# Turning the first stage's normed rows in by VectorE and DRAM instead of TensorE, in a one-core decoder layer

## The chip, the cores and the metric

One core of a Trainium2 chip runs the whole layer. The metric is the device time of one execution in microseconds. The core has five engines that each work through a queue of instructions in order: PE (TensorE, with PEld for its weight loads), DVE (VectorE), ACT (ScalarE), POOL (GpSimd) and SP (SyncE, which here only issues DMAs). They meet at semaphores.

## The reference

The input x has 16 x 256 tokens of 256 channels in float32. Three sublayers follow each other, each ending in a layer norm of `x + sublayer(x)`:

```python
# 1: attention to a fixed table, squared ReLU in place of a softmax (4 heads of 64)
n = layernorm(x) * ln_g + ln_b
q = n.reshape(B, T, 4, 64).transpose(0, 2, 1, 3)
k = w_fc.reshape(-1, 64); v = w_proj.T.reshape(-1, 64)      # 1024 x 64
p = square(relu(einsum('bhtd,sd->bhts', q, k)))
x = norm(x + (x + einsum('bhts,sd->bhtd', p, v)))
# 2: cross attention, 16 heads of 16, to ctx; a bias per head from clipped differences of `frac`
D = clip(frac[:, None, :] - frac[:, :, None], -0.2, 0.2)
attn = gamma * (Q @ K.T) / 4 + delta * (alpha_pos * max(D, 0) + alpha_neg * min(D, 0))
x = norm(x + (softmax(attn) @ V) @ Wo.T + bo)
# 3: FFN, 256 -> 1024 -> 256, with one of eight small LoRA updates chosen per token
x = norm(x + ffn(x))
```

## The kernel before

The order of work is written out by hand, and each engine's queue follows the program text. The first sublayer is the first stage. It works on eight blocks `tb` of 512 tokens, `rows_in[tb]`. The second stage (cross attention of 16 batches with the FFN of earlier blocks woven in) starts when it is through.

A block's x lies as four row tiles of 128 tokens by 256 channels. To be multiplied with the keys, the normed rows must stand with channels on the partitions. The steps for that, all done for block `tb + 1` while block `tb` is in its matmuls:

- `load` (L262) fetches x with one DMA of 512 KB; `measure` (L191, L192) takes mean and variance of the rows on DVE.
- `scale` takes the logarithm and exponential on ACT (L200, L202), and then four small DVE operations (L208 to L211, L246) for 1/std and the shift. It works on the sums of eight row tiles at once: four of the coming block, and four of an earlier block's result.
- `norm_in` (L251) writes the normed rows `xn` on ACT, four operations of 128x256.
- `turn_in(c)` turns them by eight 128x128 matmuls with an identity on TensorE (L326) into PSUM, and copies them out with `ln_g` and `ln_b` applied, on ACT for c = 0 (L330) and on DVE for c = 1 (L335), as `xnT`.

The matmuls of a block run in eight steps m, four for each half c of the channels. In a step, `scores` (L345) makes two `ps_a` tiles of 128x1024; ACT takes their ReLU into `pr` (L353), DVE squares it (L354). Then `values` (L364) multiplies the squares of the step before with the value table and adds up in two tiles of PSUM. There are two `ps_a` tiles in all, so the scores of a step need the ReLUs of the step before to be through; `pr` has four.

After each half, `keep` copies the sums out on ACT (L373, L378) and adds them on POOL (L379) as `xt`. The result of block `tb - 1` is turned back to rows by `turn_rows`: eight transposes on TensorE (L390) into a `ps_a` tile, and two DVE operations that add 2x (L396) into `y`. `measure_out` takes its statistics and `norm_out` writes the normed rows on ACT (L251) and adds a bias on POOL (L419).

Work besides the matmuls is listed in `steps[m]` and issued after the matmuls of step m. `turn_in`, `turn_rows` and the second half of `turn_in` stand in the list `turning` after step 7, that is at the boundary between two blocks:

```python
steps[6].append(lambda tb=tb: nxt.norm_in(by[tb]))
turning.append(lambda: nxt.turn_in(0))
if tb:
    turning.append(rows_in[tb - 1].turn_rows)
turning.append(lambda: nxt.turn_in(1))
```

Three side jobs lie in this stage. `clip` makes `dneg` and `dpos` of the first five batches, ten operations of 128x512 on DVE (L547) in blocks 2 to 6, at steps 0 and 5; those of batches 2 to 4 go to DRAM (L566). `biases` folds constants in block 1, with matmuls in PSUM tiles `ps_b` (L153, L160, L167). `load_cross` and `load_ffn` fetch the weights of the later sublayers during block 0.

`tile_b` hands out the `ps_b` tiles, two in turn. The second stage already has, for half of the heads of its later groups, another way of turning: `blocks` turns 32x32 blocks with a DVE operation (L707), writes them to DRAM (L712), and `fetch` reads them back in another order (four DMAs, L724).

Of the kernel before, what the change touches and what calls it, by code (L numbers as in the profile page):

```python
# [14 lines left out]
P = 128  # L15
# [7 lines left out]
def tile_decoder_layer(ctx: ExitStack, tc: tile.TileContext, a: dict, out: bass.AP):  # L23
# [214 lines left out]
    if True:  # L238
# [16 lines left out]
        class Block:  # L255
# [16 lines left out]
            def norm_in(self, by):  # L272
                self.xn = p1.tile([P, 4, C], FP, tag="xn", bufs=1, name="xn")
                for j in range(4):
                    scaled(self.xn[:, j, :], self.x[:, j, :], by, j)

            def begin(self):

                self.xn = p1.tile([P, 4, C], FP, tag="xn", bufs=1, name="xn")
                self.xnT = p1.tile([P, CC, 512], FP, tag="xnT", bufs=1, name="xnT")  # L280
                self.mv = small.tile([P, 4, 2], FP, tag="mv", name="mv")
                near, by = [], []
                for jj in range(2):
                    self.measure(jj)
                    near.append(near_root(self.mv[:, 2 * jj : 2 * jj + 2], 2))
                for jj in range(2):
                    mv = self.mv[:, 2 * jj : 2 * jj + 2]
                    by.append(scaling_of(mv, newton(mv, near[jj], 2), 2))
                for j in (0, 2, 1, 3):
                    rs, nm = by[j // 2]  # L290
                    if j < 2:
                        scaled(self.xn[:, j, :], self.x[:, j, :], (rs, nm), j)
                    else:
                        k = j - 2
                        nc.vector.tensor_scalar(
                            self.xn[:, j, :], self.x[:, j, :], rs[:, k : k + 1],
                            nm[:, k : k + 1], ALU.mult, ALU.add,
                        )
# [19 lines left out]
                        ln_b[:, c : c + 1], ALU.mult, ALU.add,  # L318
                    )

            def turn_in(self, c):
                if c == 0:
                    self.xnT = p1.tile([P, CC, 512], FP, tag="xnT", bufs=1, name="xnT")
                ps = tile_b()
                for j in range(4):
                    nc.tensor.transpose(  # L326
                        ps[:, j * P : (j + 1) * P], self.xn[:, j, c * P : (c + 1) * P], ident
                    )
                if c == 0:
                    nc.scalar.activation(  # L330
                        self.xnT[:, c, :], ps, AF.Identity,
                        bias=ln_b[:, c : c + 1], scale=ln_g[:, c : c + 1],
                    )
                else:
                    nc.vector.tensor_scalar(  # L335
                        self.xnT[:, c, :], ps, ln_g[:, c : c + 1], ln_b[:, c : c + 1],
                        ALU.mult, ALU.add,
                    )

            def scores(self, c, n):  # L340

                hf, q = divmod(n, 4)
# [1 line left out]
                for h, k in ((0, 0), (1, 1), (0, 1), (1, 0)):  # L344
                    nc.tensor.matmul(  # L345
                        sc[64 * k : 64 * k + 64, h, :],
                        lhsT=kT[64 * h : 64 * h + 64, q, hf * P + 64 * k : hf * P + 64 * k + 64],
                        rhs=self.xnT[64 * h : 64 * h + 64, c, :],
                        start=True,
                        stop=True,  # L350
                    )
                pr = p1.tile([P, 2, 512], FP, tag="pr", bufs=4, name="pr")
                nc.scalar.activation(pr, sc, AF.Relu)  # L353
                nc.vector.tensor_tensor(pr, pr, pr, ALU.mult)  # L354
                return pr

            def values(self, c, n, pr):
# [12 lines left out]
                    )  # L370

            def keep(self, c, last=False):
                nc.scalar.copy(self.oT[:, c, :], self.acc[0])  # L373
                if last:
                    nc.vector.tensor_tensor(self.oT[:, c, :], self.oT[:, c, :], self.acc[1], ALU.add)
# [51 lines left out]
    if True:  # L427
# [8 lines left out]
        class Batch:  # L436
# [119 lines left out]

            def clip(self, name):

                t = self.cut(name, *((0.0, -CLAMP) if name == "dneg" else (CLAMP, 0.0)))
# [453 lines left out]
    with tc.manual_schedule():  # L1013
# [21 lines left out]
        def scale(tb, mv):  # L1035
            by[tb] = scaling(mv, 8)

        for tb in range(NB):
            now = rows_in[tb]
            steps = [[] for _ in range(8)]  # L1040

            mv = small.tile([P, 8, 2], FP, tag="mv8", bufs=2, name="mv8")
            if tb in (0, 1, NB - 1):
                nc.vector.memset(mv, 0.0)

            if tb > 1:
                last = rows_in[tb - 2]
                last.mv = mv[:, 4:8]
                for jj in range(2):
                    steps[1 + jj].append(lambda jj=jj: last.measure_out(jj))  # L1050
                for j in range(4 if tb + 1 == NB else 1):
                    steps[7 - j // 2].append(
                        lambda j=j, tb=tb: last.norm_out(by[tb], 4 + j, j, nc.gpsimd)
                    )
            if tb > 2:
                older = rows_in[tb - 3]
                for j in range(1, 4):
                    steps[j].append(
                        lambda j=j, tb=tb: older.norm_out(by[tb - 1], 4 + j, j, nc.gpsimd)
                    )  # L1060
            turning = []
            if tb + 1 < NB:
                nxt = rows_in[tb + 1]
                nxt.mv = mv[:, 0:4]
                if tb:
                    steps[0].append(nxt.load)
                for jj in range(2):
                    steps[3 + jj].append(lambda jj=jj: nxt.measure(jj))
                steps[6].append(lambda tb=tb: nxt.norm_in(by[tb]))
                turning.append(lambda: nxt.turn_in(0))  # L1070
                if tb:
                    turning.append(rows_in[tb - 1].turn_rows)
                turning.append(lambda: nxt.turn_in(1))
            if tb + 1 < NB or tb > 1:
                steps[5].append(lambda tb=tb, mv=mv: scale(tb, mv))
# [22 lines left out]
            for m in range(8):  # L1098
# [334 lines left out]
```

## Time and profile before

| | |
|---|---|
| median of 3 runs (lowest to highest) | 887.35 us (887.11 to 888.24) |
| profiled execution, time | 887.49 us |
| profiled execution, span | 885.70 us |
| PE busy | 862.4 us, 97% of the span |
| DVE, ACT, POOL busy | 78%, 65%, 53% |
| first stage: `scores`, 1024 records (L345) | 124.6 us busy |
| first stage: `values`, 1024 records (L364) | 122.7 us busy |
| turning in (L326), 56 transposes | 8.6 us busy |
| turning out in this stage (L390 into `ps_a`), 48 transposes | 6.2 us busy |

Busy time is a union: pieces that overlap on an engine count once. The mean duration of an instruction is longer than its share, since matmuls overlap each other (a matmul of `scores` takes 593 ns from start to end, while 16 of them start within 1.72 us). The order of instructions on an engine and what each waited for is read from the timeline; `[0.95 <-ACT pr L353]` behind a row means that the engine had been idle 0.95 us and that ACT's instruction of line 353 released it.

### The profile page before, as it was taken

To read this page: it belongs to the slowest core of one execution; us is meant where nothing else is said; L and a number is where in the kernel's file an instruction comes from. 1 tells how busy PE (TensorE), PEld (TensorE's weight loads), DVE (VectorE), ACT (ScalarE), POOL (GpSimd) and SP (SyncE) were. 2 spreads that over 40 slices of the span, in tenths; PEclk is the share of its full clock that TensorE was granted. 3 is DMA by queue.
4 is the path that set the end of the run, shared out by engine and by line. 5 is a ranking of instruction groups with operands and counts; after the bars stand their busy time and mean duration, and the time that the engine had idled before them with its cause. 6 is when DMAs were issued, how large, how long until landed. Compare 5 with 4: busy or idle time off the path is not lost.

```text
span 885.7 us, 20853 instructions
## 1 busy us (share of the span) xinstructions
PE 862.4 (97%) x7708; PEld 513.1 (58%) x7708; DVE 693.3 (78%) x1975; ACT 577.0 (65%) x1012; POOL 466.6 (53%) x455
## 2 busy tenths in 40 slices
PE   8999999999999999999999999999999999999997
PEld 4334444444456776567547656754765675576655
DVE  6878899889779898769778877877887787777444
ACT  5766777777788788647747765774875577475111
POOL 1100223322479898656828765883976678374010
PEclk9999999999999999999999999999999999999999
DMA  5501101010001333454454536445453644642001
GB/s 139 159 1 43 54 24 44 31 49 1 8 8 48 99 98 110 139 162 149 158 155 150 158 129 184 151 155 168 138 164 133 193 151 135 181 149 102 28 7 41
DMA packets 70373, 92.94 MB, mean 105 GB/s; under 512 B 13824, under 2 KB 55296, under 8 KB 70272
## 3 DMA queue, kind: packets, MB, share of 16 engines
q1 hardware_dynamic: 69696, 91.35, 33.2%
q8 instruction: 61, 1.00, 0.5%
q14 instruction: 40, 0.33, 0.1%
q10 hardware_dynamic: 576, 0.26, 0.1%
HBM read 50.43 MB, written 39.58 MB: 102 GB/s over the span
## 4 chain that ended last, share of the span: by engine, by line
PE 44%; DVE 11%; issue 2%; POOL 1%; ACT 1%; DMA 0%; ACTq 0%; POOLq 0%; DVEq 0%
PE ps_l L945 9%; PE ps_b L978 6%; PE ps_l L664 5%; PE ps_v L764 5%; PE ps_b L743 4%; DVE neg L682 3%; PE ps_b L614 3%; PE ps_v L978 3%; PE ps_b L477 2%; PE ps_l L958 2%; DVE z L707 1%; PE ps_b L503 1%; PE ps_b L532 1%; POOL neg L733 1%; DVE dpos L547 1%
## 5 line engine op out<-in xcount | busy, mean ns | idle before, releaser
L682 DVE CUSTOM_DVE_ANT_0 neg<-ps_l,neg 128x256 f32<-128x256 f32 x512 | 181.5, 420 | 41.4 <-PE ps_l L664 38.3
L642 POOL TENSOR_SCALAR neg<-dneg,aneg,delta 128x512 f32<-128x512 f32 x252 | 198.9, 804 | 20.9 <-PE ps_b L743 10.0
L654 ACT ACTIVATE ps_l<-dpos,apos_d 128x512 f32<-128x512 f32 x256 | 172.2, 688 | 49.9 <-DVE mx L682 30.9
L354 DVE TENSOR_TENSOR pr<-pr 128x1024 f32<-128x1024 f32 x128 | 153.8, 1243 | 30.2 <-ACT pr L353 29.8
L733 POOL TENSOR_TENSOR neg<-neg,mx 128x1024 f32<-128x1024 f32 x65 | 124.0, 1909 | 85.4 <-DVE mx L682 84.3
L353 ACT ACTIVATE pr<-ps_a 128x1024 f32<-128x1024 f32 x128 | 125.0, 1026 | 53.0 <-PE ps_a L345 52.7
L345 PE MATMUL ps_a<-xnT,kT 64*64 64x512 f32 x1024 | 124.6, 593 | 1.0 <-ACT xnT L330 0.4
L364 PE MATMUL ps_v<-pr,vv 64*64 64x512 f32 x1024 | 122.7, 589 | 0.0
L945 PE MATMUL ps_l<-xt,wi 128*128 128x512 f32 x248 | 111.7, 596 | 0.2
L750 ACT ACTIVATE pT<-ps_b 128x512 f32<-128x512 f32 x160 | 87.4, 590 | 32.4 <-PE ps_b L743 30.9
L743 PE MATMUL ps_b<-ident,neg 128*128 128x128 f32 x640 | 87.1, 277 | 3.4 <-ACT pT L750 2.3
L743 PEld LDWEIGHTS ps_b<-ident,neg 128*128 128x128 f32 x640 | 71.5, 141 | 24.0 <-issue 6.2
L364 PEld LDWEIGHTS ps_v<-pr,vv 64*64 64x64 f32 x1024 | 45.0, 133 | 64.5 <-issue 54.6
L379 POOL TENSOR_TENSOR xt<-xt,half 128x512 f32<-128x512 f32 x15 | 19.1, 1274 | 119.8 <-ACT half L378 119.8
L419 POOL TENSOR_TENSOR hid<-hid,bo 128x256 f32<-128x256 f32 x32 | 43.6, 1366 | 71.8 <-ACT hid L251 71.8
L696 ACT ACTIVATE neg<-neg,mx 128x256 f32<-128x256 f32 x192 | 81.3, 498 | 0.0
L764 PE MATMUL ps_v<-pT,vaug 128*32 128x256 f32 x1024 | 74.3, 385 | 7.2 <-DVE x L991 6.0
L664 PE MATMUL ps_l<-kM,qT 32*64 32x256 f32 x2048 | 79.8, 388 | 0.0
L345 PEld LDWEIGHTS ps_a<-xnT,kT 64*64 64x64 f32 x1024 | 41.9, 133 | 65.3 <-issue 52.5
L945 PEld LDWEIGHTS ps_l<-xt,wi 128*128 128x128 f32 x248 | 45.6, 191 | 49.4 <-issue 44.6
L978 PE MATMUL ps_b<-wof,hT 128*128 128x256 f32 x304 | 68.4, 380 | 0.0
L524 POOL TENSOR_SCALAR kM<-keys,of_head 128x512 f32<-128x512 f32 x22 | 38.7, 1760 | 48.4 <-DVE keys L513 48.4
(137 smaller groups left out, 1183.3 us busy)
## 6 DMA issues: line engine op xcount, KB each, us to landing
pT<-away_z SPq DMA_DIRECT2D x192, 128.0 KB
away_z<-z SPq DMA_DIRECT2D x24, 512.0 KB
away_z<-kT SPq DMA_DIRECT2D x24, 512.0 KB
away_v<-raw SPq DMA_DIRECT2D x16, 512.0 KB
cT<-in_ctxT SPq DMA_DIRECT2D x16, 256.0 KB
v<-away_v SPq DMA_DIRECT2D x32, 128.0 KB
invs<-rows SPq DMA_DIRECT2D x16, 256.0 KB
x<-in_x SPq DMA_DIRECT2D x7, 512.0 KB
```

The lines of the kernel that those rows point to most:

```text
L345: nc.tensor.matmul(sc[64 * k : 64 * k + 64, h, :], lhsT=kT[64 * h : 64 * h + 64, q, hf * P + 64 * k : hf * P + 64 * k + 64], rhs=self.xnT[ ...
L353: nc.scalar.activation(pr, sc, AF.Relu)
L354: nc.vector.tensor_tensor(pr, pr, pr, ALU.mult)
L364: nc.tensor.matmul(self.acc[k][64 * h : 64 * h + 64, :], lhsT=vv[64 * k : 64 * k + 64, hf, 64 * q : 64 * q + 64], rhs=pr[64 * k : 64 * k + ...
L642: nc.gpsimd.tensor_scalar(self.neg[:, g], self.batch.dneg, aneg[:, h : h + 1], delta, ALU.mult, ALU.mult,)
L654: nc.scalar.activation(banks[g], self.batch.dpos.rearrange("p j k -> p (j k)"), AF.Copy, scale=apos_d[:, h : h + 1],)
L664: nc.tensor.matmul(banks[g][64 * h : 64 * h + 64, j * S : (j + 1) * S], lhsT=self.batch.qT[rows, self.o, j * P + 64 * h : j * P + 64 * h + ...
L682: nc.vector.tensor_tensor_reduce(out=self.t[:, g, j, :], in0=banks[g][:, j * S : (j + 1) * S], in1=self.neg[:, g, j, :], scale=-1.0 if min ...
L733: eng.tensor_tensor(rows, rows, top.to_broadcast([P, 4, S]), ALU.subtract)
L743: nc.tensor.transpose(ps[:, k * S + j * P : k * S + (j + 1) * P], self.t[:, g, j, k * P : (k + 1) * P], ident,)
L945: nc.tensor.matmul(self.banks[g], lhsT=wi[:, c, f * P : (f + 1) * P], rhs=self.xT[:, c, :], start=(c == 0), stop=False,)
L978: nc.tensor.matmul(ps[:, 0:C], lhsT=self.hT[f][:, j * P : (j + 1) * P], rhs=wof[:, f, :], start=(f == 0), stop=(f == FC - 1),)
```

## The change

The first block is turned in as before, by `turn_first`. For the other seven, `turn_in` is gone. A normed block is turned in 32x32 blocks by one DVE operation of 128x1024 (`blocks_in`), written to DRAM by one DMA and read back by four, into `xr`. Then ACT applies `ln_g` and `ln_b` in place, two operations of 128x512 (`affine`). In `xr` the tokens of a block stand in another order (by 32s), so `scores` reads it in four pieces of 128 tokens, and `keep` puts the tokens back in order as it copies.

The list of steps is laid anew. `measure` of the next block moves to steps 0 and 1, `scale` to step 2, `norm_in` to steps 2 and 3 in halves, `blocks_in` to step 4, `affine` to step 6. The load of x is issued half a block earlier, in step 4 of the block before. `turn_rows` moves from the boundary to step 3 of the next block and takes two `ps_b` tiles in place of a `ps_a` tile. `measure_out` stands in steps 5 and 6, `norm_out` in steps 5 and 7. The tile of sums has three buffers, and `xnT` two. `load_ffn` moves from block 0 to block 1, step 6.

One of the sixteen squares of a block, that of c = 0, n = 3, goes from DVE to ACT. The clips of the first five batches go from DVE to POOL, three operations for each.

```diff
+            def norm_in(self, by, jj):
+                if jj == 0:
+                    self.xn = p1.tile([P, 4, C], FP, tag="xn", bufs=1, name="xn")
+                for j in range(2 * jj, 2 * jj + 2):
+                    scaled(self.xn[:, j, :], self.x[:, j, :], by, j)
+            def blocks_in(self):
+                z = p1.tile([P, 4, CC, 4, 32], FP, tag="z", bufs=1, name="z_in")
+                nc.vector.transpose(
+                    z.rearrange("p n c j q -> p j c n q"),
+                    self.xn.rearrange("p j (c n k) -> p j c n k", c=CC, k=32),
+                )
+                away = drams.tile([P, 4, 8 * P // 4], FP, tag="rows_in", name="away_x")
+                nc.sync.dma_start(out=away, in_=z.rearrange("p n c j q -> p n (c j q)"))
+                self.xr = p1.tile([P, 4, CC, P], FP, tag="xnT", name="xr")
+                for n in range(4):
+                    nc.sync.dma_start(
+                        out=self.xr[32 * n : 32 * n + 32].rearrange("k r c e -> k r (c e)"),
+                        in_=away[:, n].rearrange("(r k) e -> k r e", k=32),
+                    )
+            def affine(self):
+                for c in range(CC):
+                    nc.scalar.activation(
+                        self.xr[:, :, c], self.xr[:, :, c], AF.Identity,
+                        bias=ln_b[:, c : c + 1], scale=ln_g[:, c : c + 1],
+                    )
-            def turn_in(self, c):
...
             def scores(self, c, n):
...
-                        rhs=self.xnT[64 * h : 64 * h + 64, c, :],
+                        rhs=(self.xr[64 * h : 64 * h + 64, :, c] if self.tb
+                             else self.xnT[64 * h : 64 * h + 64, c, :]),
...
-                nc.vector.tensor_tensor(pr, pr, pr, ALU.mult)
+                if (c, n) == (0, 3):
+                    nc.scalar.activation(pr, pr, AF.Square)
+                else:
+                    nc.vector.tensor_tensor(pr, pr, pr, ALU.mult)
...
             def keep(self, c, last=False):
-                nc.scalar.copy(self.oT[:, c, :], self.acc[0])
+                rows = tokens(self.oT[:, c, :])
+                nc.scalar.copy(rows, order(self.acc[0]))
...
-                nc.scalar.copy(half, self.acc[1])
+                nc.scalar.copy(tokens(half), order(self.acc[1]))
...
             def turn_rows(self):
-                ps = psA.tile([P, 2, 512], FP, tag="A", name="ps_a")
-                halves = [self.turn_out(jj, ps[:, jj, :]) for jj in range(2)]
+                halves = [self.turn_out(jj) for jj in range(2)]
...
             def clip(self, name):
...
+                if self.b < MADE:
+                    t = p2.tile([P, 2, S], FP, tag=name, name=name)
+                    for j in range(2):
+                        nc.gpsimd.tensor_scalar(
+                            t[:, j], self.frow, nfcol[:, 2 * self.b + j : 2 * self.b + j + 1],
+                            high, ALU.add, ALU.min,
+                        )
+                    nc.gpsimd.tensor_scalar(t, t, low, None, ALU.max)
...
+                nxt.mv = sums[tb][:, 0:4]
+                for jj in range(2):
+                    steps[jj].append(lambda nxt=nxt, jj=jj: nxt.measure(jj))
...
+                steps[2].append(lambda tb=tb: scale(tb, sums[tb]))
...
+                for jj in range(2):
+                    steps[2 + jj].append(lambda nxt=nxt, tb=tb, jj=jj: nxt.norm_in(by[tb], jj))
+                steps[4].append(nxt.blocks_in)
+                steps[6].append(nxt.affine)
+            if 0 < tb < NB - 1:
+                last = rows_in[tb - 1]
+                last.mv = sums[tb + 1][:, 4:8]
+                steps[3].append(last.turn_rows)
+                for jj in range(2):
+                    steps[5 + jj].append(lambda last=last, jj=jj: last.measure_out(jj))
+            if tb + 2 < NB:
+                steps[4].append(rows_in[tb + 2].load)
+            if tb > 1:
+                older = rows_in[tb - 2]
+                for j in range(4):
+                    steps[5 + j // 2 * 2].append(
+                        lambda older=older, j=j, tb=tb: older.norm_out(by[tb], 4 + j, j, nc.gpsimd)
+                    )
...
-                steps[2] += [load_ffn]
...
+                steps[6].append(load_ffn)
...
-            for piece in turning:
-                piece()
```

More of the change, by code (lines that the diff above doesn't have):

```diff
@@ L270, in measure @@
                     row_stats(self.x[:, j, :], self.mv[:, j, :])
-            def norm_in(self, by):
-                self.xn = p1.tile([P, 4, C], FP, tag="xn", bufs=1, name="xn")
-                for j in range(4):
+            def norm_in(self, by, jj):
+                if jj == 0:
+                    self.xn = p1.tile([P, 4, C], FP, tag="xn", bufs=1, name="xn")
+                for j in range(2 * jj, 2 * jj + 2):
                     scaled(self.xn[:, j, :], self.x[:, j, :], by, j)
+            def blocks_in(self):
[18 more added lines that the diff above has]
+                    )
             def begin(self):
                 self.xn = p1.tile([P, 4, C], FP, tag="xn", bufs=1, name="xn")
-                self.xnT = p1.tile([P, CC, 512], FP, tag="xnT", bufs=1, name="xnT")
+                self.xnT = p1.tile([P, CC, 512], FP, tag="xnT", name="xnT")
                 self.mv = small.tile([P, 4, 2], FP, tag="mv", name="mv")
@@ L319, in turn_first @@
                     )
-            def turn_in(self, c):
[L322 to L338, printed above, removed]
             def scores(self, c, n):
@@ L347, in scores @@
                         lhsT=kT[64 * h : 64 * h + 64, q, hf * P + 64 * k : hf * P + 64 * k + 64],
-                        rhs=self.xnT[64 * h : 64 * h + 64, c, :],
+                        rhs=(
+                            self.xr[64 * h : 64 * h + 64, :, c]
+                            if self.tb
+                            else self.xnT[64 * h : 64 * h + 64, c, :]
+                        ),
                         start=True,
@@ L372, in keep, with tokens, order @@
             def keep(self, c, last=False):
-                nc.scalar.copy(self.oT[:, c, :], self.acc[0])
+                def tokens(t):
+                    return t.rearrange("p (j r q) -> p r j q", j=4, q=32) if self.tb else t
+                def order(t):
+                    return t.rearrange("p (r j q) -> p r j q", r=4, q=32) if self.tb else t
+                rows = tokens(self.oT[:, c, :])
+                nc.scalar.copy(rows, order(self.acc[0]))
                 if last:
-                    nc.vector.tensor_tensor(self.oT[:, c, :], self.oT[:, c, :], self.acc[1], ALU.add)
+                    nc.vector.tensor_tensor(rows, rows, order(self.acc[1]), ALU.add)
                     return
                 half = p1.tile([P, 512], FP, tag="half", bufs=1, name="half")
-                nc.scalar.copy(half, self.acc[1])
+                nc.scalar.copy(tokens(half), order(self.acc[1]))
                 nc.gpsimd.tensor_tensor(self.oT[:, c, :], self.oT[:, c, :], half, ALU.add)
@@ L557, in clip @@
             def clip(self, name):
-                t = self.cut(name, *((0.0, -CLAMP) if name == "dneg" else (CLAMP, 0.0)))
+                high, low = (0.0, -CLAMP) if name == "dneg" else (CLAMP, 0.0)
+                if self.b < MADE:
[6 more added lines that the diff above has]
+                    nc.gpsimd.tensor_scalar(t, t, low, None, ALU.max)
+                else:
+                    t = self.cut(name, high, low)
                 if 2 <= self.b < MADE:
@@ L1036, in scale @@
             by[tb] = scaling(mv, 8)
+        sums = [small.tile([P, 8, 2], FP, tag="mv8", bufs=3, name="mv8")]
+        nc.vector.memset(sums[0], 0.0)
         for tb in range(NB):
@@ L1040, in tile_decoder_layer @@
             steps = [[] for _ in range(8)]
[L1042 to L1061, printed above, removed]
+            if tb + 1 < NB:
+                sums.append(small.tile([P, 8, 2], FP, tag="mv8", bufs=3, name="mv8"))
+                if tb + 1 in (1, NB - 1):
+                    nc.vector.memset(sums[tb + 1], 0.0)
             if tb + 1 < NB:
@@ L1063, in tile_decoder_layer @@
                 nxt = rows_in[tb + 1]
-                nxt.mv = mv[:, 0:4]
-                if tb:
-                    steps[0].append(nxt.load)
+                nxt.mv = sums[tb][:, 0:4]
                 for jj in range(2):
[L1068 to L1072, printed above, removed]
@@ L1073, in tile_decoder_layer @@
-                turning.append(lambda: nxt.turn_in(1))
-            if tb + 1 < NB or tb > 1:
-                steps[5].append(lambda tb=tb, mv=mv: scale(tb, mv))
+                    steps[jj].append(lambda nxt=nxt, jj=jj: nxt.measure(jj))
+            if tb + 1 < NB or tb > 1:
+                steps[2].append(lambda tb=tb: scale(tb, sums[tb]))
+            if tb + 1 < NB:
+                for jj in range(2):
+                    steps[2 + jj].append(lambda nxt=nxt, tb=tb, jj=jj: nxt.norm_in(by[tb], jj))
+                steps[4].append(nxt.blocks_in)
+                steps[6].append(nxt.affine)
```

## The prediction

> **What bounds the kernel now.** The changed code runs only in the first stage (matmuls L345 and L364, 9.37 to about 253 us). I cut the span into stretches first, because the page's shares mix two stages.
>
> ```profile
> core 0: us, PE busy (x) PEld busy (x) DVE busy (x) ACT busy (x) POOL busy (x), PEclk, DMA share, GB/s
> 80.00:110.00 30.00, 29.99 (x280) 13.36 (x276) 27.03 (x42) 21.81 (x31) 5.80 (x4) 1.00 0.12 40
> 110.00:140.00 30.00, 29.99 (x279) 13.18 (x273) 27.02 (x42) 22.77 (x32) 9.21 (x6) 1.00 0.13 41
> ```
>
> TensorE is busy 29.99 of 30 us at full clock: this stage ends when its matmul list ends. VectorE is next (90%), ScalarE has a quarter free, the DMA engines are nearly idle. The second stage is TensorE's too and its code is not touched, so I carry any shift of the stage's end to the end of the run.
>
> Next the timeline at one boundary between two blocks (start, duration, engine, line):
>
> ```profile
> 125.68 1.93 PE L364 MATMUL ps_v<-pr,vv 64*64 64x512 f32 x16
> 127.53 0.66 PE L326 MATMUL ps_b<-ident,xn 128*128 128x128 f32 x4
> 128.03 1.04 PE L390 MATMUL ps_a<-ident,xt 128*128 128x128 f32 x8
> 128.90 0.60 PE L326 MATMUL ps_b<-ident,xn 128*128 128x128 f32 x4
> 129.43 2.19 PE L345 MATMUL ps_a<-xnT,kT 64*64 64x512 f32 x16
> ```
>
> Steps inside a block start 3.433 us apart (136.56, 140.00, 143.43). Blocks start 29.77 apart (69.89, 99.66, 129.43), so a boundary costs 29.77 - 8 x 3.433 = 2.30 us for sixteen transposes, eight turning in and eight turning out. TensorE does not wait here; the transposes themselves are the cost.
>
> **What is removed.** The change deletes the eight L326. The eight turning out stay, alone, in step 3. A lone group of eight of this shape is L167: its step takes 60.97 - 56.29 = 4.68, so 1.25. A boundary thus falls from 2.30 to 1.25, six times, and the boundary after block 0, which has no turning out, goes altogether: 37.37 - (34.02 + 1.72) = 1.63, of which 0.43 was a wait for L330. If nothing new is late: 1.63 + 6 x 1.05 = 7.9 us.
>
> **What is added, on whose queue.** VectorE gets one transpose of 128x1024 (L707: 1.24 us) per block and loses L335 (0.81), one square (1.17, now ScalarE's, about 1.0) and, in five blocks, two clips of 0.69. It stays near 90% and gates only through the chain below. GpSimd gets ten clips: 2 x 0.56 (L845) plus 0.80 (L642) to 1.76 (L524), so 1.9 to 2.9 us each; it is idle two thirds of this stage and the clips' readers come a block or more later, so zero by itself. SP gets five issues per block (0.34 + 1.75); ahead of them stands at most a clip's write, done ten microseconds before. Behind them stand the load of x, needed four steps later, and load_ffn, moved past two blocks and needed in the second stage: zero. The rearranged reads of TensorE cost nothing: L764, some of whose inputs run in pieces of 32, takes 376 to 404 ns throughout. The rearranged ScalarE copies (0.59) have no row; not below 0.59, as the elements are the same, and up to twice that; I take 0.59, the nearest sort of row being VectorE's copy L540: it writes pieces of 16 elements and takes 0.69, what VectorE's plain copies of 128x512 out of PSUM take.
>
> **The new wait.** The rows now come back through DRAM, and `affine` stands in ScalarE's queue in step 6. ScalarE runs in order, so behind it stand the two Relus of step 7, and TensorE's first scores of the next block need the ps_a tile that the first of them frees. How ScalarE's in-order waits look today:
>
> ```profile
> 149.16 2.61 DVE L354 TENSOR_TENSOR pr<-pr 128x1024 f32<-128x1024 f32 x2
> 150.26 0.21 ACT L202 ACTIVATE near<-ln 128x8 f32<-128x8 f32 x1
> 151.70 0.15 DVE L208 SCALAR_TENSOR_TENSOR sd<-mv,near 128x8 f32<-128x8 f32 x1
> 153.24 2.07 ACT L251 ACTIVATE xn<-x,nm,rs 128x256 f32<-128x256 f32 x4
> ```
>
> The scaling finishes only when VectorE is through its squares. Before, the norming stood a step later, behind Relus; now it follows at once in ScalarE's queue and holds step 3's Relus.
>
> I followed a steady block from its first score (t=0), with rows 3.43 a step, Relu pair 1.94, first Relu 1.12 after its step's start, squares 2.33. Step 2: Relus end 10.1, the logarithm pair 10.65, squares 11.5, four small VectorE operations 12.2. First two norms to 13.3; step 3's Relus (ready at 11.6) to 15.25; squares to 16.65; the two y sums (1.28) to 17.95; step 4's squares to 20.3; the transpose z to 21.55. TensorE meanwhile: step 4 begins at 15.15, after the 1.25, with no stall.
>
> Then the trip through DRAM. The second stage makes the same trip with the same shapes:
>
> ```profile
> 355.72 1.24 DVE L707 STREAM_TRANSPOSE kT<-neg 128x1024 f32<-128x1024 f32 x1
> 356.99 0.34 SPq L712 DMA_DIRECT2D away_z<-kT  x1
> 359.75 1.28 SPq L724 DMA_DIRECT2D pT<-away_z  x3
> 363.00:363.25 0.25, 0.25 (x2) 0.16 (x1) 0.25 (x1) 0.04 (x1) 0.25 (x1) 1.00 0.20 41
> 825.59 0.60 SPq L600 DMA_DIRECT2D invs<-rows  x1
> 829.46 0.69 DVE L607 TENSOR_TENSOR oT<-v,invs 128x512 f32<-128x512 f32 x1 [4.29 <-DMA invs<-rows]
> ```
>
> Write issue to first read issue is 2.76. The four reads' last bytes move about 3.4 after the first issue (quarter-microsecond windows, last column GB/s), and an earlier write's traffic ended 0.55 before SP went on; so 4.0 to a reader, and the 256 KB read L600 reached its reader in 3.87. Sum 0.06 + 2.76 + 4.0 = 6.8 us.
>
> xr is there at 28.4. ScalarE, which came to `affine` at about 25, idles 3 us; the two operations (L647, 0.72 each, overlapping) take 1.4, to 29.8; step 7's first Relu ends 30.75; the next block starts at 30.8. TensorE's own work would let it start at 28.9. So a block takes 30.8, not 29.77: the 1.05 gained is paid for by a wait of 1.9. VectorE's spare time does not help; the chain is serial.
>
> Trainium skill, "DMA: Bandwidth & Descriptors", Anatomy of one DMA: about 2.0 us fixed plus bytes at 436 GB/s, measured on GpSimd-issued transfers. As an estimate, two passes over 512 KB are 6.4 us; the block would be 30.4 and the sum below +5 instead of +7. The rows decide.
>
> Moving work to GpSimd is not quite free: the pair of squares beside a GpSimd addition takes 2.61 against 2.33. The skill's "GPSIMD Engine Reference", Specifications, says that GpSimd's SBUF interfaces are shared with VectorE and contend with operations of two SBUF inputs, which the squares are. That agrees with the row and speaks against moving the clips.
>
> **Sum.** Block 0: the same chain from 9.37 (no turning out; norming holds TensorE 0.5 at step 4; z ends 29.05) puts block 1 at 38.3 instead of 37.37: +0.95. Block 1: L153 is a third ps_b tile behind the two of turning out and waits for a y sum that VectorE reaches late, some 2.2; its other matmuls then hide the trip; 33.95 against 32.52: +1.4. Blocks 2 to 6: 5 x (30.8 - 29.77) = +5.2. Block 7 starts without the 0.27 tail of a turn: -0.3. Together +7.3. The profiled execution took 887.49 (885.70 span and 1.79 around); that gives 894.8. It stands 0.14 above the median of the runs, so 894.6.
>
> Uncertain sizes: the trip 6.2 to 7.2 (times 6), the copies, contention on the chain (next but one): 889.5 to 898.5 in this case.
>
> **Rivals.** (A) Faster: the rows are usable before ScalarE needs them. TensorE then never waits for them, and the sum is -1.1 (block 0, with its 0.5 kept), +1.2 (block 1), 5 x -1.05, -0.3: -5.4, 882. Break-even is a trip of 5.8 us, or z ready a microsecond earlier; full gain needs 4.9. For: ScalarE's and VectorE's queues have slack I may have used up on paper, and the DMA engines are quieter than around 357 us. Against: quiet trips there show 2.7 to 2.8 for the write alone, every time.
> (B) Slower still: clips of up to 2.9 us in step 0 overlap the squares that gate the scaling. At 0.28 per 1.27 of overlap that is 0.5 per block, five times: +2.5, 897.
> (C) The trip is near the break-even, the wait eats just the gain, and the time stays at 887.4.
>
> **How the numbers follow.** A measurement of this kernel tells about 0.2% from no change. My forecast has 0.55, B 0.13, A 0.26, C 0.06. So faster 0.26, same 0.06, slower 0.68. The range takes in A's value and the upper bounds of B: 882 to 898.5.
>
> **What would show it.** Right: ScalarE idle about 3 us before `affine`, put down to the DMA into xr; TensorE idle some 1.9 us before each of blocks 3 to 7, put down to ScalarE's Relu; blocks 30.8 apart; no L326; L153 late in block 1. Wrong: blocks at 28.7 with TensorE at 29.99 of 30 (A), or a write-to-reader trip far from 6.8.

## The result, and the profile after

The changed kernel takes 908.09 us (median of 4, 905.52 to 909.61) against 887.31 (887.11 to 888.24) on the same chip: a ratio of 1.0229, 95% interval 1.0202 to 1.0256. The forecast was 894.6 with a range up to 898.5: the direction is right, the loss of 20.8 us almost three times the 7.3 forecast. The profiled execution took 909.61 (span 907.8, 22.1 longer than before). Of these 22.1, the first stage (to the first matmul into `ps_l`, at 270.75 in place of 252.88) holds 17.9, and the second, whose code is the same, 4.2. Such a split comes from one profiled execution of each kernel; the medians are over 4 runs or more.

In the answers below L281 is `blocks_in`, L286 and L289 its write and reads, L296 `affine`, L350 `scores`, L362 the Relu, L366 the square. Busy time by block, here blocks 2, 3 and 4 from first score to first score (the columns are those shown of before):

```profile
core 0: us, PE busy (x) PEld busy (x) DVE busy (x) ACT busy (x) POOL busy (x), PEclk, DMA share, GB/s
75.06:107.08 32.02, 28.98 (x269) 11.70 (x265) 25.52 (x39) 23.09 (x32) 16.39 (x10) 1.00 0.51 158
107.08:139.66 32.58, 29.08 (x265) 11.66 (x265) 25.88 (x39) 23.99 (x34) 19.74 (x12) 1.00 0.26 70
139.66:172.43 32.77, 30.71 (x264) 14.05 (x264) 25.70 (x39) 24.17 (x34) 19.63 (x12) 0.95 0.19 60
```

TensorE had 29.99 of 30 us; now it is idle 2 to 3.5 us in each of these blocks of 32 to 33, no other engine has become full, and in one of the three rows its clock falls to 0.95. The timeline of block 3's end shows the chain that fills the gap:

```profile
127.56 1.24 DVE L281 STREAM_TRANSPOSE z_in<-xn 128x1024 f32<-128x1024 f32 x1
128.83 0.32 SPq L286 DMA_DIRECT2D away_x<-z_in  x1
132.90 1.74 SPq L289 DMA_DIRECT2D xr<-away_x  x4
137.18 1.52 ACT L296 ACTIVATE xr<-xr,ln_b,ln_g 128x512 f32<-128x512 f32 x2 [5.13 <-DMA xr<-away_x]
138.60 1.91 ACT L362 ACTIVATE pr<-ps_a 128x1024 f32<-128x1024 f32 x2
139.66 2.61 PE L350 MATMUL ps_a<-xr,kT 64*64 64x512 f32 x12 [3.50 <-ACT pr L362]
```

Each row follows from the one above it: released by it, or next in ScalarE's queue. The transpose ends at 128.80, the rows are usable at 137.18: a trip of 8.38. ScalarE stands still for 5.13 us, the Relu of step 7 behind it is late, and TensorE waits 3.50. The norms ahead of it hold step 3's Relus as forecast:

```profile
119.78 1.09 ACT L251 ACTIVATE xn<-x,nm,rs 128x256 f32<-128x256 f32 x2 [2.23 <-DVE nm L246]
120.78 1.91 ACT L362 ACTIVATE pr<-ps_a 128x1024 f32<-128x1024 f32 x2
```

The same, added up over the first stage (us in total, times, longest), TensorE's waits and then ScalarE's:

```profile
PE ps_a L350 <- ACT pr L362: 16.7, 8, 3.5
PE ps_b L153 <- DVE y L415: 2.2, 1, 2.2
```

```profile
ACT xr L296 <- DMA xr<-away_x: 27.0, 7, 5.1
```

Two things had no place in the forecast. First, TensorE's granted clock (last column but two) halves after some of the gaps; block 4 begins so:

```profile
140.14:143.55 3.41, 3.41 (x21) 1.59 (x17) 2.89 (x3) 2.73 (x5) 2.46 (x2) 0.50 0.24 29
143.55:146.96 3.41, 3.41 (x36) 2.03 (x32) 2.43 (x6) 2.43 (x4) 1.41 (x2) 1.00 0.00 0
```

The same 3.41 us hold 21 matmuls in place of 36. There are four such stretches, from 58.2, 140.1, 205.0 and 529.3 us, each 3.41 long and so worth 1.7. The kernel before has none ahead of its last microseconds. Second, TensorE waits longer in the second stage for rows that come back through DRAM, 4.2 us against 0.5; the first row is of before, the second of after:

```profile
PE ps_v L764 <- DMA pT<-away_z: 0.5, 1, 0.5
```

```profile
PE ps_v L792 <- DMA pT<-away_z: 4.2, 3, 2.9
```

### The profile page after: what moved, and what is told of

Same layout as the page of the kernel before. It is cut to its first block, busy times and chain, and to the rows that moved or that the text cites. A ratio compares the mean times of both kernels' runs of the same rounds, so it can differ in the third digit from the quotient of the medians.

```text
span 907.8 us, 20825 instructions
## 1 busy us (share of the span) xinstructions
PE 863.0 (95%) x7652; PEld 510.3 (56%) x7652; DVE 689.3 (76%) x1957; ACT 589.0 (65%) x1027; POOL 519.7 (57%) x485
## 4 chain that ended last, share of the span: by engine, by line
PE 40%; DVE 10%; DMA 3%; ACT 2%; issue 2%; SPq 0%; POOL 0%; ACTq 0%; POOLq 0%; DVEq 0%
PE ps_l L973 9%; PE ps_b L1006 6%; PE ps_l L692 4%; PE ps_v L792 4%; PE ps_b L771 3%; DVE neg L710 3%; PE ps_b L642 3%; PE ps_v L1006 2%; PE ps_b L495 2%; PE ps_l L986 2%; DMA pT<-away_z 2%; DVE z L735 1%; PE ps_b L521 1%; PE ps_b L550 1%; DVE dpos L565 1%
## 5 line engine op out<-in xcount | busy, mean ns | idle before, releaser
L366 DVE TENSOR_TENSOR pr<-pr 128x1024 f32<-128x1024 f32 x120 | 150.6, 1293 | 55.2 <-ACT pr L362 55.0
L362 ACT ACTIVATE pr<-ps_a 128x1024 f32<-128x1024 f32 x128 | 124.1, 1021 | 22.3 <-PE ps_a L350 21.3
L350 PE MATMUL ps_a<-xr,kT 64*64 64x512 f32 x896 | 112.2, 609 | 16.2 <-ACT pr L362 16.2
L376 PE MATMUL ps_v<-pr,vv 64*64 64x512 f32 x1024 | 125.2, 598 | 0.0
L398 POOL TENSOR_TENSOR xt<-xt,half 128x512 f32<-128x512 f32 x15 | 23.4, 1559 | 129.5 <-ACT half L397 129.5
L350 PEld LDWEIGHTS ps_a<-xr,kT 64*64 64x64 f32 x896 | 38.2, 134 | 73.6 <-issue 40.9
L1006 PEld LDWEIGHTS ps_b<-wof,hT 128*128 128x128 f32 x304 | 57.5, 190 | 9.3 <-issue 1.6
```

Of the source, the lines that this page charges most:

```text
L350: nc.tensor.matmul(sc[64 * k : 64 * k + 64, h, :], lhsT=kT[64 * h : 64 * h + 64, q, hf * P + 64 * k : hf * P + 64 * k + 64], rhs=(self.xr[ ...
L376: nc.tensor.matmul(self.acc[k][64 * h : 64 * h + 64, :], lhsT=vv[64 * k : 64 * k + 64, hf, 64 * q : 64 * q + 64], rhs=pr[64 * k : 64 * k + ...
L1006: nc.tensor.matmul(ps[:, 0:C], lhsT=self.hT[f][:, j * P : (j + 1) * P], rhs=wof[:, f, :], start=(f == 0), stop=(f == FC - 1),)
```

## The experiments

Theory T: the serial chain of step 2 and the trip set the block, the other edits cost little. Rivals: VectorE and GpSimd contend (G); the rearranged order itself costs (L). Every time below stands beside 887.8 to 888.0 of the kernel before on the same chip (887.3 for the changed kernel). "First stage" is the start of the first matmul into `ps_l`, "second" is the rest of the span; before: 252.9 and 632.8.

**The trip taken away.** `e1_early_read`: the reads fetch rows of the input in step 0; the written rows go unused.

```diff
-    in_=away[:, n].rearrange("(r k) e -> k r e", k=32),
+    in_=rows[:, n].rearrange("(r k) e -> k r e", k=32),   # rows: of a["x"]; issued in step 0
```

> The four reads into xr fetch the raw input rows at step 0 instead of the turned rows after the write, so the result is not the layer's; every operation, DMA and byte count stays. Theory T (the trip through DRAM holds ScalarE at affine, and that holds TensorE): the wait before affine vanishes, blocks stand 28.7 to 28.9 us apart, no half-clock stretches at the boundaries, stage ends near 249 instead of 270.8 us; time 883 to 887. Rival L (the new order of steps itself, with its norms queued early on ScalarE, costs): blocks stay above 30.5, time above 895. Rival G (GpSimd's clips slow VectorE so that VectorE bounds): blocks above 30, VectorE at 95% or more.

Measured 887.43 (ratio 0.9994, 0.9985 to 1.0003), blocks 29.0 apart, clock 1.0 throughout. First stage 249.5, 3.3 shorter than before and 21.2 shorter than after, and its waits are gone but for L153's:

```profile
PE ps_b L153 <- DVE y L418: 2.2, 1, 2.2
PE ps_a L353 <- ACT pr L365: 0.5, 2, 0.3
```

The second stage took 635.7, so the gain was given back there, and the whole lies just above the 883 to 887 of T. Blocks are a little longer than T's 28.7 to 28.9, but neither rival's signs show. With the rows there early, the first stage's whole loss is gone.

**TensorE's turn put back, all else as changed.** `e2_tensor_turn`:

```diff
-    steps[4].append(nxt.blocks_in); steps[6].append(nxt.affine)
+    # after step 7:
+    nxt.turn_in(0); nxt.turn_in(1)
```

> The changed kernel with its new order of steps, clips on GpSimd and a square on ScalarE, but turned in by TensorE at the boundary as before. Theory T: no trip, so no long wait; a boundary costs two groups of eight apart, 1.25 each with a short wait for the copy out, 30.0 to 30.4 per block against 29.77; block 1 has its ps_b wait of 2.2 and perhaps one half-clock stretch; time 889 to 894. Rival L: 898 or more. If the new order were a gain by itself: below 886.

Measured 893.15 (1.0059, 1.0042 to 1.0076); first stage 258.5, second 632.8. T's 889 to 894 holds. This order without the trip loses 5.2 us: blocks are 30.35 apart, since turning in now stands alone at the boundary and its scores wait for the copies (7 times 0.4), and L153's wait of 2.2 lengthens block 1 from 32.5 to 35.5. In the changed kernel the first of these costs does not arise.

**The clips alone.** `e3_clips`: the kernel before with the new `clip` on GpSimd.

> The kernel before with only the clips of the first five batches on GpSimd, three operations each. Theory T: nothing of it is on the path, 886.5 to 888.5. Rival G: the squares beside the clips get slower (2.6 to 2.9 a pair against 2.33) and the scaling and norming at steps 5 and 6 come late: 890 or more.

Measured 889.21 (1.0015, 1.0005 to 1.0024): 1.3 us lost. The squares, mean over the middle of the first stage, before and here:

```profile
L354 DVE TENSOR_TENSOR pr<-pr 128x1024 f32<-128x1024 f32 x86 | 103.7, 1246 | 13.7 <-ACT pr L353 13.4
```

```profile
L354 DVE TENSOR_TENSOR pr<-pr 128x1024 f32<-128x1024 f32 x86 | 108.3, 1299 | 16.3 <-ACT pr L353 16.3
```

They are 4% slower beside GpSimd. The time lies between T's range and G's. But the first stage of the profiled execution is only 0.15 longer (253.03); the other 1.1 came in the second (633.9), where nothing was edited. So the slower squares are shown, and that they cost the 1.3 us is not.

**The trip started sooner.** `e4_z_step2`:

```diff
-    steps[2 + jj].append(... norm_in(by[tb], jj))
-    steps[4].append(nxt.blocks_in)
+    steps[2].append(... norm_in(by[tb], jj))
+    steps[2].append(nxt.blocks_in)
```

> The changed kernel with all four norms and the 32x32 transposes issued in step 2 instead of steps 2, 3 and 4. Theory T: z ends at about 15.8 us of the block instead of 21.6, the rows are there at 23 to 24.5 even with a slow trip, ScalarE comes to affine at 25 or later and does not wait; TensorE may wait 0.3 at step 4; blocks 28.8 to 29.4 apart, no half-clock stretch at boundaries, one in block 1; time 884 to 889. If the trip's wait were only a symptom (rival L or G): blocks stay at 31 or more, 900 or more.

Measured 897.84 (1.0103, 1.0082 to 1.0125); first stage 259.5. ScalarE no longer waits for the rows, but blocks are 30.3 apart, not 28.8 to 29.4, and the time lies between T's 884 to 889 and the rivals' 900. Four norms now hold step 3's Relus, for which TensorE waits 0.8 in a block, and a run of four squares beside GpSimd's work (the end of a clip, then an addition) takes 6.08 in place of some 4.7:

```profile
104.17 6.08 DVE L366 TENSOR_TENSOR pr<-pr 128x1024 f32<-128x1024 f32 x4
```

T holds for the wait; part of what it frees is lost to the norms' place and, as the slow squares suggest, to contention. Block 1 takes 36.6 here, with a wait of 3.6 at L153.

**The gaps filled.** `e5_fill`: two 128x128x512 matmuls in step 7 of blocks 0 to 6.

```diff
+    for q in range(2):
+        nc.tensor.matmul(tile_b(), lhsT=kT[:, q, 0:P], rhs=<this block's rows, c = 1>, start=True, stop=True)
```

> The changed kernel with two 128x128x512 matmuls into ps_b, whose results nobody reads, in TensorE's queue at the end of blocks 0 to 6. They take about 1.5 us of the gap of 2.1 to 3.5 us in which TensorE otherwise waits there. Theory T (a gap in TensorE's work is what brings the half clock): the stretches of clock 0.50 at the boundaries near 140 and 205 us go; those after the wait of L153 (58 us) and in the second stage (529 us) may stay. At about 1.7 us each that is 3.4 less: 903 to 906. Rival U (the half clock falls where it falls, whatever TensorE does): all four stay, and the time stays at 908 or rises.

Measured 906.35 (1.0195, 1.0168 to 1.0222). Idle times at the boundaries are 1.4 or less, and no half clock follows them; the same place as above:

```profile
139.01:142.42 3.41, 3.41 (x32) 1.49 (x36) 2.97 (x3) 3.41 (x5) 1.99 (x2) 1.00 0.26 40
```

The stretch after L153's wait stays, and one of the second stage has moved to 449.6, after a wait of 3.1 there. U falls: the stretches follow idle time. The total is above 903 to 906 by a little: the first stage fell by 2.3 and not by 3.4, since block 1, where TensorE does not wait for the trip, is 2.0 longer with the fill, and the second rose by 0.4.

**The instruction fetches shifted.** The DMA queues of the page name two that fetch instructions. In the changed kernel, the 4.33 us from block 0's write on, and then block 4's:

```profile
q1 hardware_dynamic: 144, 0.52, 30.5%
q8 instruction: 1, 0.02, 2.2%
```

```profile
q1 hardware_dynamic: 256, 0.63, 37.9%
```

SP's queue in the same two places, write to reads 4.08 and 2.76:

```profile
28.67 0.35 SPq L286 DMA_DIRECT2D away_x<-z_in  x1
32.75 1.73 SPq L289 DMA_DIRECT2D xr<-away_x  x4
...
163.05 0.32 SPq L286 DMA_DIRECT2D away_x<-z_in  x1
165.81 1.74 SPq L289 DMA_DIRECT2D xr<-away_x  x4
```

One packet of 16 KB lies in the longer write and none in the shorter. Queue q8 moves 61 such packets in all, about as many as TensorE's 7,652 matmuls and as many weight loads would fill at 256 instructions to a packet (59.8). The write leg below is the time from the write's issue to that of the first read. `e6_shift`:

```diff
-WARM = 30   # transposes of 128 columns
+WARM = 54   # matmuls of 64 columns
```

> The changed kernel with 54 warm-up matmuls of 64 columns in place of 30 of 128 ahead of block 0: the same time there, but 48 more instructions of TensorE, so that its packets of instructions are fetched some 2.7 us earlier against the work of the first stage. Theory F (a packet of instructions that is fetched during the write of away_x holds one DMA engine up): the write legs of blocks 0 and 1, 4.08 and 3.60 us with a packet of queue q8 inside, fall to 2.75; that of block 3 (4.07, with a packet of q14) stays. Block 0 gets 1.3 shorter; the time 905 to 908, the lower end if a half-clock stretch goes as well. Rival S (the slow legs belong to these blocks' own traffic): 4.08 and 3.60 stay.

Measured 930.94 (1.0487). The edit misjudged its own cost: the 54 matmuls are 108 records of 0.2 us, and block 0 starts 18 us late (27.4 in place of 9.3). The question is answered all the same. Write legs of blocks 0 to 6 were 4.08, 3.60, 2.75, 4.07, 2.76, 2.77, 2.70; they are 2.66, 2.78, 4.17, 3.70, 3.39, 2.78, 2.69, and the long legs again are those with a packet inside. S falls. Blocks 0 and 1 have their packet in the read instead (5.4 us after the write's issue) and take 8.40 and 8.74 in all.

Over the six kernels in which ScalarE waited for the rows (after, e5, e6, e7, e12, e13) there are 42 trips. 23 had a packet of either queue that started between 0.2 us before and 1.7 after the write's issue, or 4.0 to 5.4 after: 7.42 to 8.74, mean 8.08. Of the other 19, 18 took 6.82 to 7.29, mean 7.05; one took 7.92 and has no explanation here, since its packet at 6.0 stands where four other trips with one took 7.01 to 7.12. These bounds were set after the trips had been seen; that the long legs moved with the packets in `e6_shift` is the test. A packet at the wrong moment goes with 1.0 us more.

The Trainium skill, "Runtime: NRT & Kernel Launch", Instruction fetch mechanics, has instructions refilled in blocks of 16 KiB, 256 instructions, and calls the cost of crossing a block mostly hidden. The size agrees with the 61 packets. TensorE itself does not wait for the fetch (before, it is busy 29.99 of 30 us with such packets at 85.2 and 101.6), but a transfer on which one falls takes the 1.0 us more.

**The second stage.** Is it the place of the new DRAM tile (P) or when the fetches fall (F)? `e7_shared` takes the tile from the buffers that the second stage uses; `e10_spare` gives the kernel before a tile that nobody uses.

```diff
-    away = drams.tile(..., tag="rows_in", name="away_x")
+    away = drams.tile(..., tag="blocks", name="away_x")      # e7
+    spare = drams.tile([P, 4, 8 * P // 4], FP, tag="rows_in", name="spare")   # e10, twice, 4 KB written
```

> The changed kernel with its DRAM tile taken from the same two buffers as the second stage's trips, so that all DRAM tiles lie where they lie in the kernel before. Theory P (the new tile's place in DRAM slows the second stage's trips): the time after the first stage falls from 637.0 to about 633, and the whole to 904 to 905; the slow write legs there go from 12 of 30 to about 6. Rival F (these legs are slow by when instructions are fetched and transfers meet, which the order of the first stage shifts): still about 637, and 907 to 909.

> The kernel before, with two buffers of a further DRAM tile of 512 KB each ahead of the others, into which 4 KB are written once at the start and which nobody reads; no trip, no other order. Theory P: the time after the first stage rises from 632.8 to 636 or 637, with waits of TensorE for rows out of away_z of some 4 us, and the whole to 890.5 to 892. Rival F: 632 to 634, and 887 to 888.5.

e7: 902.86 (1.0165, 1.0150 to 1.0180), second stage 633.2, as P had it; but the first stage was 3.6 shorter too (a half-clock stretch less, trips 0.3 shorter), which P does not explain. e10: 888.07 (1.0003, 0.9994 to 1.0012), second stage 633.4, as F had it: a further tile by itself does nothing to the kernel before.

Three more runs test F. `e13_dummy` puts 56 transposes without a reader back into the changed kernel; `e14_warm` adds 72 warm-ups to the kernel before; `e15_trip_own` gives the kernel before the DRAM trip, unread.

```diff
+    steps[7].append(nxt.fill)        # e13: eight transposes of xn into two tiles ps_b
-WARM = 30
+WARM = 102                           # e14
+    steps[6].append(nxt.trip)        # e15: xn to away_x, four reads into a spare tile
```

> The changed kernel with the 56 transposes that it took out put back as dummies at the same place (the end of blocks 0 to 6), their results read by nobody. TensorE's number of instructions in the first stage is then that of the kernel before again. Theory F (packets of instructions that are fetched during the second stage's trips delay them, and 112 fewer instructions of TensorE moved all later fetches against the trips): the time after the first stage falls from 637.0 to 633 to 634.5, with waits of TensorE for rows out of away_z of 1 us or less in place of 4.2; the boundaries, whose gaps the dummies shorten by 1.2, show at most one half-clock stretch; 901.5 to 904.5. Rival (the second stage is slower through the trips' traffic or tile): 636 to 637.5 after the first stage, 904 to 907.

> The kernel before with 102 warm-up transposes in place of 30. They start the blocks 72 x 0.19 = 13.6 us later, and add 144 instructions of TensorE, which by packets of 256 is the same shift as 112 fewer. Theory F: the time after the first stage rises from 632.8 to 635 or more, with waits of TensorE for rows out of away_z of 2.5 us or more in place of 0.5; 903.5 to 906. Rival: 632.5 to 633.5 and 0.5 to 1, 901 to 902.

> The kernel before, in which the normed rows of seven blocks are also written to a DRAM tile of their own and read back by four DMAs into a tile that nobody reads; TensorE's transposes turn them in as before. Theory F: the DMAs cost nothing by themselves, 633 after the first stage and 887 to 889 in all. Rival (traffic or tile of the trip slow the second stage): 636 or more after the first stage, and 890.5 or more.

TensorE's wait in the second stage, e13 and then e14:

```profile
PE ps_v L800 <- DMA pT<-away_z: 0.9, 1, 0.9
```

```profile
PE ps_v L764 <- DMA pT<-away_z: 4.3, 3, 2.1
```

e13's second stage takes 633.35, e14's 637.1 with a half-clock stretch at 518.6: both as F said beforehand, one in each direction. e15 is at 888.53 (1.0008, 0.9998 to 1.0018) with 633.8, so trip and tile of its own add at most 1.0 here. F's totals were missed: e13 took 907.25 (1.0215), since with the old count the packets fell on the trips of blocks 4 and 6 (8.67 and 8.15) and the boundaries kept two half-clock stretches; e14 took 899.45, its warm-ups 0.11 apart and not 0.19.

All kernels with TensorE's old count (before, e2, e3, e10, e13, e15) have a second stage of 632.8 to 634.0. Those whose fetches are shifted by 112, or in e14 by 144 the other way, which to packets of 256 is the same (after, e1, e4, e7, e8, e9, e11, e12, e14), have 633.2 to 637.5. But the count does not decide alone. The wait that makes most of the difference stands 255 to 259 us into the second stage. It is absent with the old count, 1.75 to 2.9 in the shifted kernels whose trip has a DRAM tile of its own (after, e1, e4, e8, e12), and 0.4 or less where that tile is shared with the second stage (e7, e9, e11). The row of e7, whose longest wait stands at another place, 101 us in:

```profile
PE ps_v L792 <- DMA pT<-away_z: 1.7, 2, 1.3
```

e14, with no further tile, has 2.1 at that place. So the count of instructions matters, as e13 and e14 forecast, and in the shifted kernels the place of the tile does too, as P had it. How the two act together was not isolated, and the cause of the second stage's 4.2 stays open to that extent.

**The wait of L153.** `e12_later`: `steps[m + 3]` in place of `steps[m + 2]` for the four pieces of `biases`.

> The changed kernel with the folding of constants in block 1 one step later (steps 3 to 6), so that L153 no longer waits for the y sum behind two tiles of turning out. By the prediction's step for block 1, its other matmuls and that wait hide the trip; without the wait TensorE meets the trip at the boundary instead. So L153 waits for nothing, a wait of 1 to 2 us shows ahead of block 2, and block 1's 35.6 loses 0.5 to 2, of which 1.7 would be the half-clock stretch at 58 us: 905.5 to 908. Rival: the wait at L153 comes on top of everything, and 3.5 to 4 us are saved, 904 to 904.5.

Measured 902.38 (1.0164, 1.0148 to 1.0179): 5.7 less than the changed kernel, first stage 266.2. No wait replaced L153's. The rival was right: block 1 is 3.8 shorter (31.8 in place of 35.6), so the 2.2 and the stretch of half clock behind it were on top of everything. Most of the rest of the 5.7 lies in the second stage (634.2).

**A version that starts early enough.** `e8_sooner` takes the statistics half a block earlier; `e9_best` also shares the DRAM tile; `e11_best_pool` is e9 with the clips on GpSimd.

```diff
+    steps[6 + jj].append(far.measure(jj))           # rows of block tb + 2, in block tb
+    steps[0].append(scale)                          # from block 1 on; block 0: step 2
+    steps[1 + jj].append(nxt.norm_in(by[tb], jj))
+    steps[3].append(nxt.blocks_in)                  # ahead of turn_rows
...
+    steps[6 + c].append(nxt.affine(c))
+    steps[m + 3].append(next(output))               # biases; clips on VectorE, steps 0 and 2
```

> The changed kernel, with the statistics of a block's rows taken half a block sooner (steps 6 and 7 of the block before), scaling in step 0, norming in steps 1 and 2, the transpose and the write in step 3, the affine operations one in step 6 and one in step 7, the constants one step later and the clips on VectorE as in the kernel before (steps 0 and 2). Theory T (the serial chain and the trip set the block): the transpose ends some 15.5 us into a block, the rows are back by 24 even after a trip of 8.4, ScalarE and TensorE wait for no DMA, and blocks come 28.7 to 29.1 apart; the first stage ends at 247 to 250.5. With 633 to 636 after it and 1.8 around the span, 882 to 888. Rival V (VectorE, with the clips and the transposes, becomes the bound): blocks 29.8 or more apart, 890 or more.

> The run with the statistics taken sooner, its DRAM tile now from the same two buffers as the second stage's trips. Theory P (a further DRAM tile slows the second stage's trips by its place): the time after the first stage falls from 637.5 to 633, and the whole from 884.8 to 880 to 881.5. Rival F (the timing of that stage has other causes): 884 to 886.

> The run before the last with the clips of the first five batches on GpSimd (steps 0 and 2 as there). Theory G (GpSimd's clips slow VectorE's squares, but that costs only where a chain waits for VectorE): here the rows are back early, so blocks stay within 0.3 us of those with the clips on VectorE, and the whole within 2 us of that run, rather above it. Rival (moving the clips is a gain, as it frees 1.4 us of VectorE per block): 1 us or more below it.

e8: 884.78 (0.9958, 0.9938 to 0.9978), first stage 245.55, second 637.45 with a half-clock stretch at 503.8. e9: 882.27 (0.9940, 0.9924 to 0.9957), 246.0 and 634.2. Blocks 2 and 3 of e9:

```profile
85.00:113.65 28.65, 28.65 (x268) 10.55 (x264) 26.40 (x41) 23.89 (x34) 6.81 (x6) 1.00 0.25 80
113.65:142.30 28.65, 28.65 (x268) 10.60 (x264) 26.40 (x41) 23.86 (x34) 6.81 (x6) 1.00 0.23 80
```

TensorE is never idle in these blocks, VectorE at 92% does not bind (V falls), and the rows have 8.3 us or more to come back. e9 beats the kernel before by 5.6 us. The totals do not tell e9 from e8 (881.3 to 883.95 against 881.17 to 886.61), and e9's lies between P's range and F's. e11: 883.35 (0.9946, 0.9931 to 0.9960), blocks up to 0.9 us longer (29.5, more than G allowed). It is 1.1 above e9 in the median, with ranges that overlap: moving the clips is no gain even here. In blocks 2 to 4 of e11 the write of the rows also leaves 1.8 us after the transpose ends (85.49 and 87.32 in block 2): ahead of it in SP's queue stands the write of a clip that GpSimd finishes only at 86.84. The prediction had that clip's write done ten microseconds before, which holds for the changed kernel (28.64 and 28.67, 128.80 and 128.83).

## Why the prediction was wrong

**Right.** The chain: the transpose ended 21.6 to 21.7 us into blocks 2, 3 and 5 (21.55 forecast); 23.4 in blocks 4 and 6, which begin at half clock. ScalarE waits for the rows, step 7's Relu stands behind, TensorE last. The affine pair delays the Relu by 1.4. L153 waits 2.19 (2.2). Step 3's place for turning out costs TensorE no stall. The rearranged copies take 0.59, as chosen. Rival A's blocks of 28.7 did come where the rows were early: 28.65 in e9, 29.0 in e1. That e9 takes 882.3, rival A's 882, is partly luck: its first stage gains 6.9 where A added up 5.4, with constants moved and clips left on VectorE, and its second stage gives back 1.4. e1, which keeps the changed order and only has its rows early, takes 887.4.

**Failed, the term for the trip.** "Sum 0.06 + 2.76 + 4.0 = 6.8 us", bounded by 7.2, with the write "2.7 to 2.8 for the write alone, every time". It was not every time in the trace of before either: one of its writes in the second stage, at 421.4, took 3.61 to its reads, and six of 30 took over 3. I had read quiet ones. Measured were 8.34, 7.92, 7.92, 8.38, 6.94, 7.06 and 7.23: over 42 trips the undisturbed one is 7.05, and one with a packet 1.0 longer. The page's 6.4, named in the prediction, is further off than the rows. Seven trips exceed 6.8 by 6.2 us together.

**Failed, a missing term.** The step "the wait of 1.9" priced TensorE's idle time as idle time alone. Three of the seven gaps of over 2 us in the first stage brought 3.41 us at half clock, 1.7 each, 5.1 together. This is a second price on the same wait.

**Failed, "The second stage ... its code is not touched, so I carry any shift of the stage's end to the end of the run."** It gave 4.2 more: 3.7 of waits and a half-clock stretch of 1.7, with 1.2 less elsewhere. Same code was not the same timing. With TensorE's old count of instructions it took 633.3 again (e13), and with the DRAM tile shared 633.2 (e7); both matter in these profiles, and how they act together stays open.

Block by block, the excess over before's periods (us):

| block | 0 | 1 | 2 | 3 | 4 | 5 | 6 | 7 | sum |
|---|---|---|---|---|---|---|---|---|---|
| forecast | 0.95 | 1.4 | 1.03 | 1.03 | 1.03 | 1.03 | 1.03 | -0.3 | 7.3 |
| measured | 2.17 | 3.08 | 2.25 | 2.81 | 3.00 | 1.48 | 3.29 | -0.14 | 17.9 |
| trip over 6.8 | 1.54 | 1.12 | 1.12 | 1.58 | 0.14 | 0.26 | 0.43 | | 6.2 |
| half clock | | 1.7 | | | 1.7 | | 1.7 | | 5.1 |

In block 1 TensorE does not wait for the trip, so that entry does not count there; the others add up to the measured row within 0.4 in every block. In all, 7.3 of the forecast, 5.1 of longer trips, 5.1 of half clock and 4.2 of the second stage make 21.7 of the 22.1.

**Mis-sized without effect.** A clip on GpSimd takes about 5 us (two parts of 1.6 to 1.9 and one of 1.5 to 2.0), not 1.9 to 2.9. Rival B priced its contention at 2.5; moving the clips cost 1.3 in e3 and 1.1 in e11 against e9, neither of which is shown to be contention alone.

## What to carry to other kernels

Before a transfer replaces work on the engine that sets the time, start it so early that its worst trip fits, not its usual one: here 8.7 against 7.05. Turning in through DRAM cost 20.8 us as it was placed; started some 6 us sooner, with the constants moved, the clips left on VectorE and the tile shared, it gained 5.6. Price a gap in TensorE's work twice, once as idle time and once as the half clock that may follow. And read a duration from all its rows; the six long writes of thirty were in the trace.

## What was not expected of the hardware

**When the clock halves.** In nine profiles with such stretches, all onsets within one execution lie whole multiples of 3.413 us apart (24, 43 and 138 in the changed kernel). So I cut each profile into windows of that length that end 0.2 us before an onset, and added up TensorE's idle time in each. 21 of the 22 windows ahead of a stretch hold 2.1 to 3.1 us of it, one holds 1.8; of some 2,300 others none holds more than 2.08. The 0.2 us is a choice and not a measurement; without it the border lies at 2.0, with 19 of the 22 above it and no other. One stretch, in `e6_shift`, lasted two windows though the second followed 1.55 us of idle time. The length of a gap does not decide: one of 3.10 at 36.4 us, cut in two by a window's edge, had no effect, one of 2.17 at 201.5 did. The windows of these two gaps (TensorE's busy time stands after their length) hold 1.18 and 1.92 us of idle time, and 2.17:

```profile
34.13:37.54 3.41, 2.23 (x24) 0.52 (x16) 0.00 (x0) 0.56 (x1) 0.00 (x0) 1.00 0.91 259
37.54:40.95 3.41, 1.49 (x16) 0.66 (x20) 1.51 (x2) 3.03 (x5) 0.00 (x0) 1.00 0.11 37
201.38:204.79 3.41, 1.24 (x16) 0.50 (x16) 1.13 (x1) 3.41 (x5) 1.39 (x1) 1.00 0.48 166
```

The Trainium skill, "TensorE: Matmul & The Clock Gate", What's actually happening, gives the window: 4096 cycles, 3413 ns, free-running, and half rate after an idle one. Length and free running agree. That the window must be idle does not: about 2.1 of its 3.41 us suffice here. A change that leaves gaps of 2 to 3 us therefore varies by where they fall.

**Fetches and transfers.** A 512 KB write with a 16 KB packet of instructions inside took up to 1.4 us longer (4.17 against 2.75), and edits of TensorE's instructions ahead of a place move the packets: with 72 more warm-ups at the start of the kernel before (144 instructions), the second stage, 250 us later, took 4.3 us longer. Its start moved by 7.6 us as well.
